# Query projection of a perceiver block: its first group moved ahead of the branch, with a new order of fetches

## The chip, the cores and the metric

The kernel runs on one core of a Trainium2 chip. The metric is the device time of one execution in microseconds; three runs of the kernel before gave a median of 925.47 us (925.44 to 926.23). The core's engines are TensorE (PE, with its weight loads PEld), VectorE (DVE), ScalarE (ACT), GpSimd (POOL) and SyncE (SP). SP does no arithmetic here: it issues transfers. ACT can issue transfers as well.

## What is computed

One perceiver block on 32 sequences of 64 tokens of width 512, all in f32: a cross-attention over a context of 1601 rows with a mask, a causal self-attention, and a feed-forward with ternary weights. Each is added to its input. The change touches the first of the three:

```python
mn = _rmsnorm(mem_seq, rms_scale)
xn = _rmsnorm(x, rms_scale)             # x comes in already layer-normed
q = jnp.einsum('BTD,NDH->BTNH', xn, q_w)          # 4 heads of 128
kv = jnp.einsum('BSD,cKDH->cBSKH', mn, kv_w)
q = _apply_rope(q, q_pos) * HEAD_DIM ** (-0.5)
k = _apply_rope(k, k_pos)
logits = jnp.einsum('BTKGH,BSKH->BKGTS', q, k)
masked = jnp.where(mem_mask[:, None, None, None, :], logits, MASK_FILL)
probs = jax.nn.softmax(masked, axis=-1)
enc = jnp.einsum('BKGTS,BSKH->BTKGH', probs, v)
return jnp.einsum('BTNH,NHD->BTD', enc, out_w)    # added to x
```

## The kernel before, in words

**Opening (L262 to L358).** The kernel first ranks the 32 sequences by how many of their context rows are not masked. A copy turns the mask to f32 (L308), two matmuls count (L314), DVE compares the counts with `steps` (L321) and reduces them to a rank (L330 to L343), two matmuls put the ranks in order (L345, L346), and `ints` receives the order and the flag `fits` (L352, L353). Beside that the query weights `wq` are scaled, and their column mean taken away: `each` (L292), four matmuls `wmean` (L297), four DVE operations in place (L301). `wq` and the later output weights share the tile `wo`. POOL scales `wkv` (L358).

**Branch.** If the ranks fit a fixed plan of lengths (they do in this profile), `cross_last` runs, which reads only the last rows that each sequence needs, two sequences to a pair, 16 pairs; otherwise `cross_all`. Every engine loads `fits` and branches.

**Queries (`query_steps`, L193 to L252).** The 2048 tokens are taken in four groups of 512. For group g: four raw tiles `xres[2..5]` give mean and variance on DVE (`spread_of`, L207 and L208, four pairs), `deviations` (L214 on DVE, L215 on POOL) turns them into a factor per token, `tables` makes four diagonal blocks `eye` on DVE (L221), spreads them over all partitions by a matmul with ones (`rb`, L223), and multiplies the result with cosine and sine (L225, L226). Each of the four heads is four matmuls (L248) of `wq` with `wide(g)`, the transposed tokens in `xres[8..11]` or `[12..15]`. `rotate` then copies the halves across on ACT (L231, L232) and has three DVE operations (L234 to L236), the last of which writes `qT_all`. `eye` shares its place, `xres[6]`, with the cosine table, so the next group's `eye` is made after the last rotation that reads the table. Each f32 matmul is two instructions in the trace.

**Order.** `cross_last` interleaves by hand: group 0, group 1, group 2 with `project(0, j)` (keys and values of pair 0, L486) after each head, group 3. After them come `inverse_rms(1)` (L468 on DVE, L469 on POOL) and `add_mask(1)`, then the loop over pairs. Its first stage, p = 1, runs `project(1, 0..2)`, `turn_keys(0)`, `project(1, 3)`, `logits(0, 0)` (L528), `project(1, 4)`. Results of `project` leave PSUM through ACT with the pair's `rstd` (L493). SP is one queue in order: it issues `ct` and mask (`load_rest`), tokens, context rows `nat` (`load_rows`, 8 buffers, freed by `square` on ACT), the queries of a pair back from `qT_all` (`fetch_queries`), the output weights, and pieces of the feed-forward weights, whose absolute sums `magnitude` takes on DVE (L1035). `in_order` pins the program order of the named engines.

Of the kernel before, what the change touches and what calls it, by code (L numbers as in the profile page):

```python
# [80 lines left out]
def perceiver_kernel(ctx: ExitStack, tc: tile.TileContext, a: dict, out: bass.AP):  # L81
# [91 lines left out]

    GQ = 4 * P

    def raw(t):
        return xres[:, 2 + t % 4]
# [4 lines left out]
    def fetch_wide(g, queues):  # L182
        src = a["xT"].rearrange("(c p) t -> p c t", p=P)[:, :, g * GQ : (g + 1) * GQ]
        for k, queue in enumerate(queues):
            part = slice(k * DC // len(queues), (k + 1) * DC // len(queues))
            queue.dma_start(wide(g)[:, part], src[:, part])

    def fetch_raw(t):
        nc.sync.dma_start(raw(t), x_in[t * P : (t + 1) * P, :])

    def query_steps(psq, psr, pool):

        S8 = GQ // T  # L193
        qcos = pool.tile([P, T], F32, name="qcos")
        qsin = pool.tile([P, T], F32, name="qsin")
        nc.sync.dma_start(qcos, a["qcos"])
        nc.sync.dma_start(qsin, a["qsin"])
        cosr, sinr = (xres[:, k].rearrange("p (b t) -> p b t", t=T) for k in (6, 7))
        eye = xres[:, 6].rearrange("p (t q) -> p t q", q=P)
        over = lambda v: v.unsqueeze(1).to_broadcast([P, S8, T])  # L200
        mvs, rss = {}, {}

        def spread_of(g, k):
            if k == 0:
                mvs[g] = small.tile([P, 4, 2], F32, tag="qmv", name=f"qmv_{g}")
            st = small.tile([P, 6], F32, tag="stats", name=f"stats_q{g}_{k}")
            nc.vector.bn_stats(st, raw(4 * g + k))  # L207
            nc.vector.bn_aggr(mvs[g][:, k], st)  # L208

        def deviations(g):  # L210


            rs = small.tile([P, 4], F32, tag="qrs", name=f"qrs_{g}")
            nc.vector.tensor_scalar(rs, mvs.pop(g)[:, :, 1], 1.0 + 1e-6, 1e-11, ALU.mult, ALU.add)  # L214
            nc.gpsimd.tensor_tensor(rs, rs, neghalf[:, :4], ALU.pow)  # L215
            rss[g] = rs

        def tables(g):
            rs = rss.pop(g)
            for k in range(4):  # L220
                nc.vector.tensor_scalar(eye[:, k], ident, rs[:, k : k + 1], None, ALU.mult)  # L221
            rb = psr(f"rb_{g}")
            nc.tensor.matmul(rb, ones, xres[:, 6], start=True, stop=True)  # L223
            rb = rb.rearrange("p (b t) -> p b t", t=T)
            nc.vector.tensor_tensor(cosr, rb, over(qcos), ALU.mult)  # L225
            nc.vector.tensor_tensor(sinr, rb, over(qsin), ALU.mult)  # L226

        def rotate(g, h, ps):
            u = pool.tile([P, S8, T], F32, tag="u", name=f"qu_{g}_{h}")
            t = norm.tile([P, D], F32, tag="xn", name=f"qt_{g}_{h}")  # L230
            nc.scalar.copy(t[:H], ps[H:])  # L231
            nc.scalar.copy(t[H:], ps[:H])  # L232
            t = t.rearrange("p (b t) -> p b t", t=T)
            nc.vector.tensor_tensor(u, ps.rearrange("p (b t) -> p b t", t=T), cosr, ALU.mult)  # L234
            nc.vector.tensor_tensor(t, t, sinr, ALU.mult)
            nc.vector.tensor_tensor(qT_all[:, S8 * g : S8 * (g + 1), h, :], u, t, ALU.add)  # L236

        groups = NT // 4
        for g in range(groups):
            if g == 0:  # L240
                for k in range(4):
                    spread_of(0, k)
                deviations(0)
            mid, made = (2 if g == 0 else 1), []
            for h in range(NH):
                ps = psq(h, f"q_{g}_{h}")
                for c in range(DC):
                    nc.tensor.matmul(  # L248
                        ps, wq[:, c, h, :], wide(g)[:, c], start=(c == 0), stop=(c == DC - 1)
                    )  # L250
                made.append((h, ps))
                if h == mid:  # L252
                    tables(g)
                if h >= mid:
                    for k, ps in made:
                        rotate(g, k, ps)
                        if g + 1 < groups:
                            spread_of(g + 1, k)
                    made = []
                if h == NH - 1 and g + 1 < groups:  # L260
                    deviations(g + 1)
                yield  # L262


    with ExitStack() as st:
        r1 = st.enter_context(tc.tile_pool(name="r1", bufs=1))
        ps_r = st.enter_context(tc.tile_pool(name="ps_r", bufs=2, space=PSUM))
        ps_w = st.enter_context(tc.tile_pool(name="ps_w", bufs=1, space=PSUM))
        m8 = r1.tile([P, B, NC], U8, name="m8")
        table = r1.tile([B, 5, B], F32, name="table")  # L270
        steps = r1.tile([B, 2, NC], F32, name="steps")

        nc.scalar.dma_start(m8, a["maskE"])
        nc.scalar.dma_start(scale1, a["rms"])
        for c in range(DC):
            (nc.scalar if c % 2 else nc.sync).dma_start(
                wq[:, c], a["L0_xattn_q_w"].rearrange("h (c p) k -> p c h k", p=P)[:, c]
            )
        nc.scalar.dma_start(steps, a["steps"])
        nc.scalar.dma_start(table, a["rank"])  # L280
        fetch_wide(0, [nc.sync, nc.scalar, nc.sync, nc.scalar])
        for t in range(4):
            fetch_raw(t)
        for k in range(2):
            nc.scalar.dma_start(
                wkv[:, :, k], a["L0_xattn_kv_w"][k, 0].rearrange("(c p) h -> p c h", p=P)
            )
        nc.vector.tensor_scalar(scale1, scale1, 1.0, None, ALU.add)

        def centre_weights():  # L290
            each = r1.tile([P, DC, P], F32, name="each")
            nc.vector.tensor_scalar(  # L292
                each, scale1.unsqueeze(2).to_broadcast([P, DC, P]), 1.0 / D, None, ALU.mult
            )
            mean = ps_w.tile([P, D], F32, name="wmean")
            for c in range(DC):
                nc.tensor.matmul(  # L297
                    mean, each[:, c], wo[:, c], start=(c == 0), stop=(c == DC - 1)
                )
            for c in range(DC):  # L300
                nc.vector.scalar_tensor_tensor(  # L301
                    wo[:, c], wo[:, c], scale1[:, c : c + 1], mean, ALU.mult, ALU.subtract
                )

        def ranks():

            mf = r1.tile([P, B, NC], F32, name="mf")
            nc.vector.tensor_copy(mf, m8)  # L308

            halves = r1.tile([B, B, 2, NC], F32, name="halves")  # L310
            for k in range(2):
                part = slice(k * T, (k + 1) * T)
                count = ps_r.tile([P, B, NC], F32, tag="r", name=f"count_{k}")
                nc.tensor.matmul(  # L314
                    count[:B].rearrange("p b c -> p (b c)"),
                    ones[part, :B],
                    mf[part].rearrange("p b c -> p (b c)"),
                    start=True,
                    stop=True,
                )  # L320
                nc.vector.scalar_tensor_tensor(  # L321
                    halves[:, :, k],
                    count[:B],
                    0.0,
                    steps[:, k].unsqueeze(1).to_broadcast([B, B, NC]),
                    ALU.is_gt,
                    ALU.mult,
                )
            need = r1.tile([B, B], F32, name="need")
            nc.vector.tensor_reduce(need, halves.rearrange("p b k c -> p b (k c)"), AX.X, ALU.max)  # L330

            key = r1.tile([B, B], F32, name="key")
            nc.vector.scalar_tensor_tensor(key, need, float(B), table[:, 0], ALU.mult, ALU.add)
            own = r1.tile([B, B], F32, name="own")
            nc.vector.tensor_tensor(own, key, table[:, 1], ALU.mult)
            mine = r1.tile([B, 1], F32, name="mine")
            nc.vector.tensor_reduce(mine, own, AX.X, ALU.add)
            above = r1.tile([B, B], F32, name="above")
            nc.vector.tensor_scalar(above, key, mine, None, ALU.is_gt)
            rank = r1.tile([B, 1], F32, name="rank")  # L340
            nc.vector.tensor_reduce(rank, above, AX.X, ALU.add)
# [37 lines left out]
    def cross_last():  # L379
# [63 lines left out]
        def load(p):  # L443
            load_rest(p)
            load_rows(p, range(tiles(p)))
# [1212 lines left out]
```

## Time and profile before

| | us |
|---|---|
| median of three runs | 925.47 |
| the profiled execution | 926.73 |
| its span, first to last instruction | 924.5 |
| PE busy (4518 matmul instructions) | 889.0 |
| DVE, ACT, POOL busy | 630.9, 371.4, 70.9 |
| mean granted PE clock | 0.991 |
| transfers, whole span | 87.92 MB, mean 95 GB/s |

The profiled execution is 1.26 us above the median, and 2.2 us of it lie outside the span. A row of the timeline gives start, length, engine, line, operation, result and operands, and in brackets the idle time of the engine before it and what ended it. In the tables by stretch the busy time of each engine stands with the granted clock (1.00 is full speed) and the share and rate of the transfer engines.

### The profile page before, as it was taken

What the parts mean: (1) busy time and instruction counts of PE and PEld (TensorE: products, weight loads), DVE (VectorE), ACT (ScalarE), POOL (GpSimd) and SP (SyncE); (2) the same over time, 40 slices, a digit from 0 to 9 for tenths busy, and PEclk for the clock granted to TensorE, in tenths of its full rate; (3) what the DMA queues carried; (4) which work ended last, traced back from release to release, by engine and by line L of the source; (5) the groups of instructions that cost most, each with busy time, mean ns of one, the idle gap of its engine ahead of it and who ended that gap; (6) DMA issues with size and microseconds to landing.
All of it is one profiled execution on the core that took longest, in us unless ns stands there. A gap on an engine that the chain in (4) does not pass through costs nothing.

```text
span 924.5 us, 12905 instructions
## 1 busy us (share of the span) xinstructions
PE 889.0 (96%) x4518; PEld 633.5 (69%) x4518; DVE 630.9 (68%) x1215; ACT 371.4 (40%) x790; POOL 70.9 (8%) x83
## 2 busy tenths in 40 slices
PE   6799999999999998999999999999999999999997
PEld 2355777777777765666676666666668878878886
DVE  5587566565456563478898898877866775886864
ACT  0424645554455532122222322223554555554551
POOL 2010211111111100000000000000001000000000
PEclk8999999999999999999999999999999999999999
DMA  8874898777557560011111001000000020020111
GB/s 258 248 222 129 246 254 250 219 244 228 174 174 222 146 216 26 1 35 35 47 51 41 24 24 46 24 24 1 1 1 1 0 46 1 1 46 1 23 23 51
DMA packets 63123, 87.92 MB, mean 95 GB/s; under 512 B 11172, under 2 KB 34248, under 8 KB 63048
## 3 DMA queue, kind: packets, MB, share of 16 engines
q1 hardware_dynamic: 59648, 84.79, 31.2%
q10 hardware_dynamic: 3400, 2.20, 0.8%
q8 instruction: 38, 0.62, 0.3%
q14 instruction: 37, 0.30, 0.1%
HBM read 78.58 MB, written 4.19 MB: 90 GB/s over the span
## 4 chain that ended last, share of the span: by engine, by line
PE 71%; DVE 21%; issue 3%; ACT 3%; DMA 1%; POOL 1%; ACTq 0%; DVEq 0%; POOLq 0%
PE y L1465 13%; PE kvp L486 13%; PE fh L1122 11%; PE xo L608 6%; PE aV L1212 5%; PE q L248 4%; DVE s L1260 4%; PE enc L592 4%; PE lgp L528 3%; DVE amx L1269 2%; DVE s L1270 2%; DVE s L1280 2%; DVE atot L1278 2%; PE aptp L1290 1%; PE sc L1255 1%
## 5 line engine op out<-in xcount | busy, mean ns | idle before, releaser
L486 PE MATMUL kvp<-wkv,ct 128*128 128x256 f32 x576 | 135.0, 380 | 1.8 <-ACT kv L493 1.7
L486 PEld LDWEIGHTS kvp<-wkv,ct 128*128 128x128 f32 x576 | 106.9, 190 | 23.9 <-issue 9.3
L1465 PE MATMUL y<-wp,hTh 128*128 128x512 f32 x236 | 94.4, 400 | 0.4 <-DVE xres L1442 0.4
L1465 PE MATMUL y<-wp,hTl 128*128 128x512 f32 x236 | 92.8, 393 | 0.0
L1122 PE MATMUL fh<-fxh,wf 128*128 128x512 f32 x256 | 71.6, 401 | 1.3 <-DVE mv_f L128 0.9
L1122 PE MATMUL fh<-fxl,wf 128*128 128x512 f32 x256 | 70.5, 397 | 0.0
L493 ACT ACTIVATE kv<-kvp,rstd 128x256 f32<-128x256 f32 x72 | 34.0, 472 | 89.6 <-PE kvp L486 80.4
L1130 ACT ACTIVATE bank<-fh 128x512 f32<-128x512 f32 x64 | 38.1, 596 | 78.7 <-PE fh L1122 78.7
L248 PE MATMUL q<-xres,wo 128*128 128x512 f32 x128 | 59.8, 623 | 2.4 <-DVE wo L301 2.4
L1317 PE MATMUL aout<-bank,aoT 128*128 128x512 f32 x128 | 60.9, 620 | 1.1 <-ACT aoT L1311 1.1
L1200 PE MATMUL aWQ<-axT,bank 128*128 128x256 f32 x256 | 58.0, 380 | 2.9 <-POOL wo L1166 1.8
L535 DVE CUSTOM_DVE_ANT_0 pr<-lgp,bias 128x384 f32<-128x384 f32 (+6 forms) x64 | 28.4, 458 | 47.4 <-PE lgp L528 47.0
L1200 PEld LDWEIGHTS aWQ<-axT,bank 128*128 128x128 f32 x256 | 48.5, 190 | 15.4 <-issue 6.2
L608 PE MATMUL xo<-wo,encT 128*128 128x512 f32 x128 | 57.9, 594 | 1.1 <-ACT encT L601 1.1
L1460 DVE SCALAR_TENSOR_TENSOR hTl<-bank,lnw,hTh 128x512 fp32r<-128x512 f32 x59 | 44.0, 750 | 20.7 <-ACT hTh L1459 20.7
L1200 PE MATMUL aWK<-axT,bank 128*128 128x256 f32 x256 | 57.9, 379 | 0.0
L1212 PE MATMUL aV<-bank,axT 128*128 128x512 f32 x128 | 57.6, 594 | 0.0
L1122 PEld LDWEIGHTS fh<-fxl,wf 128*128 128x128 f32 x256 | 48.3, 189 | 11.2
L1122 PEld LDWEIGHTS fh<-fxh,wf 128*128 128x128 f32 x256 | 46.7, 188 | 13.2 <-issue 2.2
L1465 PEld LDWEIGHTS y<-wp,hTh 128*128 128x128 f32 x236 | 44.3, 188 | 14.0 <-DVE xres L1442 3.4
L1200 PEld LDWEIGHTS aWK<-axT,bank 128*128 128x128 f32 x256 | 48.6, 190 | 6.6
L1273 ACT ACTIVATE s<-s 128x1024 f32<-128x1024 f32 x16 | 16.9, 1058 | 90.2 <-DVE s L1270 90.2
(164 smaller groups left out, 1487.9 us busy)
## 6 DMA issues: line engine op xcount, KB each, us to landing
nat<-in_ctx_dram SPq DMA_DIRECT2D x64, 256.0 KB, 4.4
ct<-in_ctxT_dram SPq DMA_DIRECT2D x7, 768.0 KB, 4.4
xres<-in_x_dram SPq DMA_DIRECT2D x16, 256.0 KB, 4.7
xres<-in_x_dram SPq DMA_DIRECT2D x32, 128.0 KB, 5.6
qs<-bank SPq DMA_DIRECT2D x32, 128.0 KB, 4.8
raw_g<-in_W_fcT_dram SPq DMA_DIRECT2D x16, 256.0 KB, 4.5
raw_g<-in_W_projT_dram SPq DMA_DIRECT2D x16, 256.0 KB, 4.5
raw_q<-in_W_fcT_dram SPq DMA_DIRECT2D x16, 256.0 KB, 2.9
```

What stands on the lines that cost most here:

```text
L248: nc.tensor.matmul(ps, wq[:, c, h, :], wide(g)[:, c], start=(c == 0), stop=(c == DC - 1))
L486: nc.tensor.matmul(ps.rearrange("p k h -> p (k h)"), cts[p][:, c, j * P : (j + 1) * P], wkv[:, c].rearrange("p k h -> p (k h)"), start=(c ...
L592: nc.tensor.matmul(encs[s], kv[row : row + w, j, 1], pT[row : row + w, j], start=(done == 0), stop=(done + w == n),)
L608: nc.tensor.matmul(o, encT[:, h].rearrange("p s t -> p (s t)"), wo[:, h, :], start=(h == 0), stop=(h == NH - 1),)
L1122: nc.tensor.matmul(ps, wf[:, c, cols], part[:, c, :], start=(i == 0 and c == 0), stop=(i == 1 and c == DC - 1),)
L1130: nc.scalar.activation(g, ps, AF.Gelu)
L1200: nc.tensor.matmul(ps[:, m, :], ws[w][:, c, (m0 + m) * P : (m0 + m + 1) * P], xT[:, c, :], start=(c == 0), stop=(c == DC - 1),)
L1212: nc.tensor.matmul(ps, xT[:, c, i * P : (i + 1) * P], ws["WV"][:, c, :], start=(c == 0), stop=(c == DC - 1),)
L1260: nc.vector.scalar_tensor_tensor(s[half], sc[half, :, :, half].rearrange("p r m k -> p (r m) k"), DK**-0.5, cmask[half].unsqueeze(1).to_br ...
L1317: nc.tensor.matmul(ps, oT[:, c, :], ws["WO"][:, c, :], start=(c == 0), stop=(c == DC - 1))
L1460: nc.vector.scalar_tensor_tensor(lo, g, w, hi.bitcast(F32), ALU.mult, ALU.subtract)
L1465: nc.tensor.matmul(y, part[:, t, :], wp[:, c, :], start=(c == 0 and i == 0), stop=(c == FC - 1 and i == 1),)
```

## The change

The first group of queries, with all its tables and rotations, and the statistics and tables of group 1, now stand in the opening, ahead of the branch. The opening's PSUM pools are four banks for heads, two for `wmean` and `rb`, two for the ranks, at the places where `cross_last` has its pools. `eye` moves to `xres[0]` and the rotation's scratch to `xres[1]`; `diagonals` makes `eye` on ACT, for the next group, in the middle of the present one. `each` and the scaling of `wkv` go from DVE and POOL to ACT. The mask, the ranking table and the steps come in one transfer (`opening`); `xT`, `wq` and `wkv` are laid out by the host so that each partition reads one run. The raw tiles come in two transfers of two tiles each. In `cross_last`, the rows of a pair are fetched ahead of its `ct`, the tokens of pairs 0 and 1 only at the end of stage p = 1, `inverse_rms(1)` moves into group 2, and the loads of the output weights and of the first two pieces move into stage p = 1. The pieces' sums then run two later, to p = 16. The opening is pinned on SP too.

The core of the diff:

```diff
+    eye, turn = xres[:, 0], xres[:, 1].rearrange("p (b t) -> p b t", t=T)
-    def fetch_raw(t):
-        nc.sync.dma_start(raw(t), x_in[t * P : (t + 1) * P, :])
+    def fetch_raw(g):
+        for k in (0, 2):
+            src = x_in[(4 * g + k) * P : (4 * g + k + 2) * P, :]
+            nc.sync.dma_start(xres[:, 2 + k : 4 + k], src.rearrange("(t p) d -> p t d", p=P))
+    def diagonals(g):
+        rs = rss.pop(g)
+        for k in range(4):
+            part = slice(k * P, (k + 1) * P)
+            nc.scalar.activation(eye[:, part], ident, AF.Copy, scale=rs[:, k : k + 1])
+    def tables(g, qrot, rb):
+        nc.tensor.matmul(rb, ones, eye, start=True, stop=True)
...
+        for g in range(1, GROUPS):
+            more = g + 1 < GROUPS
+            if g > 1:
+                tables(g, qrot, psr(f"rb_{g}"))
             for h in range(NH):
+                rotate_query(g, h, query(g, h, psq(h, f"q_{g}_{h}")))
+                if more and h < 2:
+                    spread_of(g + 1, 2 * h)
+                    spread_of(g + 1, 2 * h + 1)
+                if more and h == 1:
                     deviations(g + 1)
+                if more and h == 2:
+                    diagonals(g + 1)
+                yield g, h
...
+        nc.sync.dma_start(opening, a["opening"])
         nc.scalar.dma_start(scale1, a["rms"])
+        for k in (0, 2):
+            nc.sync.dma_start(wo[:, k : k + 2], a["wq"][:, k : k + 2])
+        nc.vector.tensor_copy(mf.rearrange("p b c -> p (b c)"), m8)
+        nc.vector.tensor_scalar(scale1, scale1, 1.0, None, ALU.add)
+        nc.scalar.activation(
+            each, scale1.unsqueeze(2).to_broadcast([P, DC, P]), AF.Copy, scale=1.0 / D
+        )
+        fetch_wide(0, [nc.scalar, nc.scalar])
+        nc.scalar.dma_start(wkv, a["wkv"])
+        fetch_raw(0)
+        qrot = fetch_rotations(r1)
...
+        query(0, 0, heads[0])
...
+        for k in range(4):
+            spread_of(0, k)
+        deviations(0)
+        diagonals(0)
         for c in range(DC):
+            nc.scalar.activation(wkv[:, c], wkv[:, c], AF.Copy, scale=scale1[:, c : c + 1])
+        query(0, 1, heads[1])
+        fetch_raw(1)
+        fetch_wide(1, [nc.sync])
+        for k in range(4):
+            spread_of(1, k)
+        deviations(1)
+        query(0, 2, heads[2])
+        tables(0, qrot, ps_b.tile([P, GQ], F32, tag="b", name="rb_0"))
+        query(0, 3, heads[3])
+        for h in range(NH):
+            rotate_query(0, h, heads[h])
+            if h == 1:
+                diagonals(1)
+        tables(1, qrot, ps_b.tile([P, GQ], F32, tag="b", name="rb_1"))
+        in_order(begin, (Engine.PE, Engine.DVE, Engine.Activation, Engine.Pool, Engine.SP))
...
+        few = NATS - tiles(0)
+        load_rows(0, range(tiles(0)))
+        fetch_raw(2)
+        fetch_wide(2, [nc.sync])
+        load_rest(0)
+        load_rows(1, range(few))
+        for g, h in queries:
+            if (g, h) == (1, 1):
+                fetch_raw(3)
+                load_rest(1)
                 for j in range(tiles(0)):
                     square(0, j)
+                load_rows(1, range(few, tiles(1)))
+            if (g, h) == (1, 2):
+                inverse_rms(0)
+                add_mask(0)
+            if (g, h) == (1, 3):
+                fetch_wide(3, [nc.sync])
+            if g == 2:
+                for j in range(h * tiles(0) // NH, (h + 1) * tiles(0) // NH):
+                    project(0, j)
+            if (g, h) == (2, 1):
                 for j in range(tiles(1)):
                     square(1, j)
+                load_rows(2, range(tiles(2)))
+            if (g, h) == (2, 2):
+                inverse_rms(1)
+                add_mask(1)
+            if (g, h) == (2, 3):
+                cts.pop(0)
+                rotate(0)
+                load_rest(2)
         fetch_queries(0)
-        tc.keep_in_program_order(load_output_weights())
-        for j in range(2):
-            magnitude(j, load_piece(rawp, j, "g"))
...
             if now:
-                fetch_queries(p)
                 free = min(later, NATS - ahead)
                 if later:
                     load_rows(p + 2, range(free))
-                raws = [load_piece(rawp, j, "g") for j in (2 * p, 2 * p + 1)]
+                if p == 1:
+                    load_output_weights()
+                fetch_queries(p)
+                raws = [load_piece(rawp, 2 * p - 2 + k, "g") for k in range(2)]
...
+            if p <= NT:
+                for k, r in enumerate(raws):
+                    magnitude(2 * p - 2 + k, r)
...
                 if later:
                     load_rest(p + 2)
+                if p == 1:
+                    for v in range(4):
+                        load_tokens(v // 2, v % 2, sequence(v))
                 if p == NT - 1:
+                    raws = [load_piece(rawp, 2 * p + k, "g") for k in range(2)]
                     load_attention_weights()
```

## The prediction

> **What bounds the kernel now.** I read the summary first, then the table by stretch, then the timeline of the first 120 us. PE is busy nearly throughout; in the 40 slices (23.1 us each) only the first two lie below 9, and the first alone has a lowered clock.
>
> ```profile
> PE 889.0 (96%) x4518; PEld 633.5 (69%) x4518; DVE 630.9 (68%) x1215; ACT 371.4 (40%) x790; POOL 70.9 (8%) x83
> PE   6799999999999998999999999999999999999997
> PEclk8999999999999999999999999999999999999999
> ```
>
> So what can be won lies in about the first 95 us. The table by stretch (us; busy time and count of PE, PEld, DVE, ACT, POOL; granted clock, share and GB/s of the transfers) shows it: PE idles 8.75 us in the first stretch and 4.63 in the third, and runs at 0.80 in the second; from 100 us on it idles 0.24 us in 40.
>
> ```profile
> 0.00:15.30 15.30, 6.55 (x17) 1.95 (x17) 7.27 (x23) 0.00 (x0) 0.70 (x6) 0.95 0.79 245
> 15.30:28.25 12.95, 12.95 (x24) 5.56 (x25) 4.45 (x14) 3.60 (x5) 4.66 (x5) 0.80 0.92 284
> 28.25:45.90 17.65, 13.02 (x29) 5.44 (x28) 13.08 (x27) 7.53 (x16) 1.01 (x1) 0.96 0.73 236
> 100.00:140.00 40.00, 39.76 (x182) 30.33 (x182) 28.39 (x79) 22.28 (x66) 6.95 (x7) 1.00 0.92 262
> ```
>
> The timeline names the waits. The first head starts at 15.29, behind a chain that begins with a small transfer (`steps`, landed at 8.9 though issued at 3.29), runs through DVE and ends with `ints`. The next table matmul waits 4.63 us for `eye`, and `project(1, 2)` waits 1.71 us for the scale of pair 1.
>
> ```profile
> 8.95 1.08 DVE L321 SCALAR_TENSOR_TENSOR halves<-count,steps 32x416 f32<-32x416 f32 x2 [3.95 <-DMA steps<-in_steps_dram]
> 14.12 0.13 DVE L353 CAST ints<-fit 1x1 int32<-1x1 f32 x1
> 15.29 13.13 PE L248 MATMUL q<-xres,wo 128*128 128x512 f32 x24 [2.43 <-DVE wo L301]
> 28.25 1.02 PE L223 MATMUL rb<-xres,ones 128*128 128x512 f32 x2
> 44.21 1.92 PE L223 MATMUL rb<-xres,ones 128*128 128x512 f32 x2 [4.63 <-DVE xres L221]
> 45.93 11.40 PE L248 MATMUL q<-xres,wo 128*128 128x512 f32 x24
> 57.17 1.89 PE L486 MATMUL kvp<-wkv,ct 128*128 128x256 f32 x8
> 89.83 3.62 PE L486 MATMUL kvp<-wkv,ct 128*128 128x256 f32 x16
> 95.15 1.99 PE L486 MATMUL kvp<-wkv,ct 128*128 128x256 f32 x8 [1.71 <-ACT kv L493]
> 99.45 1.67 PE L528 MATMUL lgp<-kT,qs 128*128 128x448 f32 x4
> ```
>
> At full clock one matmul instruction of 512 columns starts 0.43 us after the last (weight loads from 21 to 39 us). The 24 from 15.29 to 28.25 took 12.96 instead of 10.3: **2.6 us of slow clock**. After the idle 4.63, the two `rb` took 1.72 instead of 0.86 and the next 24 took 11.24 instead of 10.3: **1.8 us**. I follow one mark, the first `lgp`, at 99.45.
>
> **Part 1: the opening.** Added up on the rows: the mask landed 2.52 us after its issue; with the tables beside it I take 3.4 (absolute). DVE: cast 0.38, `scale1` 0.17, to 4.0. `each` is now ACT's first operation, so the table load (1.28, the row at 21.64, which there too came after the wait) stands before it: 5.3, and 0.6 for 512 columns: 6.0. If the load runs early this is 4.7, but then the second half of `wq` (0.15 + 1.05 MB at 0.35 MB/us from 2.3) holds `wmean` to about 5.7, so 0.3 at most is won. The eight `wmean` instructions need 3.4 us warm and up to 5.4 if the clock stays low to 10; they end at 9.7 to 11.4, and 0.1 + 0.66 later the first corrected block lets the heads start: **10.6 to 12.3; I take 11.5**. The tokens: `fetch_wide(0)` stands on ACT behind `each`; issued from 6.0, behind 3.3 MB in all at 0.28 to 0.38 MB/us (the rates from 3 to 13 us), its halves land near 10.4 and 11.7, and are needed at 11.5 and 13.2. So: 15.29 - 11.5 = **3.8 us gained**, and the rank chain, `fits` and `ints` leave the path: they lie beside the heads. PE now idles under 2 us between `wmean` and the heads, where it idled 4.7; the clock should hold: **2.6 gained** (none, if it falls).
>
> **Part 2: the table gap.** `eye` of group 1 is made in the opening, so the 4.63 and its 1.8 go: **6.4 gained**. What is late next is `eye` of group 2, made behind DVE's backlog. From DVE's first `wo` correction at 10.7: corrections 2.7, fit and `ints` 0.6, four statistics 3.3, `deviations` 0.2, to 17.5. The raw pairs of group 1 can be issued on SP only when two statistics are done (15.7 and 17.4), and land 3.5 later (the shortest landing 2.0, and 0.52 MB at 0.35): statistics from 19.2 to 22.5, 22.7 with `deviations`. `rb_0` is done then (11.5 + 24 x 0.43 + 0.9 = 22.7). Tables 1.2, four rotations of 1.92 (30.52 to 32.44) 7.7, tables 1.2, DVE's own branch 0.4, two rotations each with two statistics 2 x 3.56, `deviations` 0.2: 40.5. POOL 1.1. Four `diagonals` on ACT: no row, but Exp of 128 x 128 takes 392 ns and a 128 x 256 copy 364, so 0.37 each, 1.5: `rb_2` at 43.1. PE arrives at 11.5 + 32 x 0.43 + 4 x 0.43 + branch 0.6 + 32 x 0.43 = 41.3. **A gap of 1.8 comes back.** DVE moves with PE's start, so this hardly depends on 11.5; bounds 0 and 2.5. `eye` moved off DVE is 0.9 a group there; ACT has idle time for it (7.5 busy of 17.65), and for `wkv` (4 x 0.47, beside the heads).
>
> Does the gap cost clock? In the trace 4.63 us of idling brought a slow stretch, and 1.71 at 93.4 none (1.00 in every us from 92 to 102); 1.8 lies by the second. [...] By the longer gap's row 1.8 would be added; I leave it out of the sum and keep it in the range.
>
> **Part 3: the branch in mid-stream.** From `ints` (14.25) to SP's next transfer 0.74, to PE's next weight load 1.0. PE's sequencer can run ahead under `rb_1`, so between 0 and 1.0: **0.6 lost**. Behind it `q(1, 0)` writes a bank that rotation (0,0) has left (about 25); heads 1, 2, 3 need banks left by rotations (0,2), (0,1), (0,3), at 28 to 31, before they are due.
>
> **Part 4: pair 0 to p = 1.** From group 2 on PE needs 5.16 us a head and DVE 3.6, so nothing waits. The factor of pair 1 is ready a group early: from the end of `q(3,3)` to `lgp` it was 9.62 (89.83 to 99.45), and the work in it is 4 x 1.73 + 0.55 = 7.5: **2.1 gained**. What is late next is `qs`, read back from `qT_all`: last rotation 3.4 after the last head (93.26 less 89.83), transfers of 2.0 to 4.5 after issue: the first half at 5.5, just in time; by the upper end 0.5 is lost.
>
> **Part 5: transfers and the rest, at nothing.** SP's order past the branch: rows of pair 0, raw and wide of group 2, `ct_0`, rows of pair 1: some 7.4 MB from 17.5, at 0.35 by 39; `ct_0` is needed at 48, `wide(2)` at 43. `raw(3)`, `ct_1`, `wide(3)` follow from 37 and are needed from 49 on. `fetch_queries(0)` blocks SP as before; behind it rows, output weights, `qs`, pieces and `ct_3` make 4.8 MB, 18 us at 0.28, and `ct_3` is due 22 us after `qT_all` is done. The tokens of pairs 0 and 1, 0.5 MB (1.9 us), now fall into that busy stretch (share 0.92); SP waits there 8.0 us in 80 for PE to free `ct`, so there is room, but if not it costs up to 1.9. The two late sums (1.27 on DVE at p = 16) lie in a 2.9 us idle of DVE before 354.17; the attention weights are issued about 14 us later on SP, after 343, and 4.7 MB at 0.33 bring the first by 350, where they are needed at 363.7 (times of the trace before).
>
> **The sum**: -3.8 - 2.6 - 6.4 + 1.8 + 0.6 - 2.1 = **-12.5 us**. The profiled execution, 926.73, would be 914.2; on the median of 925.47 it is **913.0**.
>
> **Rivals.**
> 1. *No gap comes back* (DVE faster than its rows, start at 10.6): 1.8 and 0.9 more, 910.3. For it: DVE's chain has 1.7 of pure waiting for raw pairs. Against: every other link is a measured row.
> 2. *The new PSUM pools wait for the old as a whole*, so that the change doesn't do what its banks are laid out for: `q(1,0)` waits for DVE's last table at 33 instead of 27.5; the gap at `rb_2` shrinks by 1.8, and an idle of 5.5 brings 1.8 of slow clock: +5.5, 918.5. For it: nothing in the trace shows a pool's hand-over. Against: in the trace before, `wkv` is scaled on POOL from 15.39 to 19.0 while PE is past the branch, so waits cross it one by one.
> 3. *Slow clock remains* in group 0 or after `rb_2`: +1.8 to 2.6, 915 to 915.6.
> 4. *Slower: transfers become the bound* in pairs 1 to 4. By 140 us 31.7 MB were moved (the table's rates); PE would want them by 127.5, 254 GB/s from 2.5 us on. While busy at 0.92 they gave 262, and SP holds `ct` back for buffers. If the mean is only 228 (that of the first 160 us), they take 139 and all is given back; below 228 the kernel is slower, at 220 by 4 us (930). Against: the rate reaches 400 in unhindered stretches, and 31% of the first 95 us is unused.
>
> **How the numbers follow.** Forecast (911.5 to 914.8) 0.52; rival 1 (909 to 911.5) 0.13; rival 3 0.12 and rival 2, with losses on transfers, together up to 919.5, 0.12; most of the gain given back but still faster 0.04; within 0.2% (1.85 us, what a measurement of this kernel can tell from no change) 0.03; rival 4 0.04. The low end is the start at 10.6, no gap, no branch cost and an early table load (913.0 - 0.9 - 1.8 - 0.6 - 0.3 = 909.4, rounded down); the high end rival 2 with half of the token cost.
>
> **What would show it.** Right: first head at 10.6 to 12.3, clock 1.00 through group 0; `rb_1` with no idle; `rb_2` with 0 to 2.5 idle, released by ACT's `eye`; no wait before `project(1, 2)`; first `lgp` near 87, and PE over 99% busy from there. Wrong: `q(1,0)` released by DVE, PE waiting for a transfer (`ct`, `nat`, `qs`), or the same 40 us after 100 showing more idle than 0.3.

## The result and the profile after

The changed kernel takes 920.2 us in the median of four runs (917.5 to 920.37), the kernel before 925.46: a ratio of 0.9929, interval 0.9916 to 0.9942. It is faster, by 5.3 us on the medians; 12.5 were forecast, with a likely band of 911.5 to 914.8 and rivals up to 919.5. The median of 920.2 lies 0.7 above all of it; by the ratio (0.9929 of 925.47 is 918.9) the time lies just inside, where rival 2 was put. The profiled execution after is the shortest of the four, 917.5 us with a span of 915.7.

First the lines of the summary that were read before:

```profile
PE 884.7 (97%) x4518; PEld 632.3 (69%) x4518; DVE 628.4 (69%) x1198; ACT 378.7 (41%) x811; POOL 67.1 (7%) x79
PE   7899999999999999999999999999999999999997
PEclk9999999999999999999999999999999999999999
```

The work of PE is the same (4518 instructions), and the first two slices are fuller, but still not full. Then the same four stretches of the table, with the same columns:

```profile
0.00:15.30 15.30, 9.84 (x23) 3.63 (x24) 8.42 (x25) 1.91 (x2) 0.70 (x6) 1.00 0.74 254
15.30:28.25 12.95, 12.71 (x30) 5.32 (x28) 9.79 (x23) 7.63 (x18) 2.04 (x2) 1.00 0.90 302
28.25:45.90 17.65, 13.62 (x28) 6.04 (x29) 12.59 (x23) 6.94 (x15) 0.00 (x0) 0.90 0.81 269
100.00:140.00 40.00, 39.76 (x179) 29.40 (x178) 26.36 (x69) 20.27 (x58) 5.91 (x6) 1.00 0.90 253
```

In the first stretch PE is busy 9.84 instead of 6.55, in the second it gets through 30 instructions at full clock instead of 24 at 0.80. The third is where the gain stops: PE idles 4.03 of 17.65, nearly as long as the 4.63 before, and the clock is lower (0.90 against 0.96). From 100 to 140 PE idles 0.24 us, as before. PE's timeline says what the third stretch waits for:

```profile
5.60 5.06 PE L314 MATMUL wmean<-wo,each 128*128 128x512 f32 x8 [0.56 <-DMA wo<-in_wq_dram]
12.32 10.54 PE L231 MATMUL q<-xres,wo 128*128 128x512 f32 x24 [1.46 <-DMA xres<-in_xT_dram]
22.70 1.02 PE L224 MATMUL rb<-xres,ones 128*128 128x512 f32 x2
26.99 1.02 PE L224 MATMUL rb<-xres,ones 128*128 128x512 f32 x2
32.27 15.67 PE L231 MATMUL q<-xres,wo 128*128 128x512 f32 x32 [4.26 <-DVE xres L240]
48.97 1.13 PE L224 MATMUL rb<-xres,ones 128*128 128x512 f32 x2 [1.03 <-ACT xres L215]
85.17 5.34 PE L502 MATMUL kvp<-wkv,ct 128*128 128x256 f32 x24
92.51 1.67 PE L544 MATMUL lgp<-kT,qs 128*128 128x448 f32 x4
```

`rb_1` (26.99) follows without idle: the table gap is gone. Behind it stands a new one of the same size: `q(1,0)`, the first head beyond the branch, waits 4.26 us for a DVE operation of line 240, the first of a rotation. DVE's timeline tells which rotation:

```profile
24.96 0.68 DVE L240 TENSOR_TENSOR xres<-q,xres 128x512 f32<-128x512 f32 x1
31.33 0.69 DVE L240 TENSOR_TENSOR xres<-q,xres 128x512 f32<-128x512 f32 x1
39.09 0.69 DVE L240 TENSOR_TENSOR xres<-q,xres 128x512 f32<-128x512 f32 x1 [4.54 <-ACT qt L238]
```

The first row is the first operation of line 240 and belongs to rotation (0,0); that of 31.33 is the fourth, belongs to rotation (0,3), and ends at 32.02, 0.25 before PE starts. The bank that `q(1,0)` writes was left by rotation (0,0), which had read it by 25.7. The last row shows the price on the other side: DVE then idles 4.54 until `q(1,0)` is there. The mark, the first `lgp`, comes at 92.51 instead of 99.45, 6.94 earlier. Nearly all of the rest of the 8.8 in the span is one slow stretch of PE's clock, 1.7 us, that the profile before has at 682 to 686 and this one has not.

Such stretches make one run differ from the next, so the experiments below are compared by their medians and ratios to runs of the kernel before on the same chip, and by marks inside the first 100 us.

### The profile page after: what moved, and what is told of

The parts are those of the page before. It is cut to its first block, busy times and chain, and to the rows that moved or that the text cites. A ratio compares the mean times of both kernels' runs of the same rounds, so it can differ in the third digit from the quotient of the medians.

```text
span 915.7 us, 12886 instructions
## 1 busy us (share of the span) xinstructions
PE 884.7 (97%) x4518; PEld 632.3 (69%) x4518; DVE 628.4 (69%) x1198; ACT 378.7 (41%) x811; POOL 67.1 (7%) x79
## 4 chain that ended last, share of the span: by engine, by line
PE 73%; DVE 21%; ACT 3%; issue 1%; DMA 1%; POOL 0%; ACTq 0%; DVEq 0%; POOLq 0%
PE kvp L502 14%; PE y L1481 13%; PE fh L1138 11%; PE xo L624 6%; PE aV L1228 5%; PE q L231 5%; DVE s L1276 4%; PE enc L608 4%; PE lgp L544 3%; DVE amx L1285 2%; DVE s L1286 2%; DVE s L1296 2%; DVE atot L1294 2%; PE aptp L1306 2%; PE sc L1271 1%; PE pt L593 1%
## 5 line engine op out<-in xcount | busy, mean ns | idle before, releaser
L1311 ACT COPY wo<-aptp 64x256 f32<-64x256 f32 x64 | 23.3, 365 | 72.2 <-PE aptp L1306 55.0
```

## The experiments

**1. The same kernel again**, for a second profile and five more runs. No edit.

> The changed kernel, unchanged, several times over. Its four runs were 917.5 once (mean clock 0.997, the profiled one) and 920.1 to 920.4 three times (0.992). Theory A: the two levels are the place of the slow-clock stretches only; a stretch is about 3.4 us long and costs 1.7 to 1.9 us, so the runs fall on levels some 1.8 to 2.7 apart, the lower clock always with the longer time, and a profiled execution near 920 shows one or two slow stretches more than the one at 32 to 36 us, at the same order of work. Rival: another wait comes and goes (a transfer); then the longer execution shows more idle PE at the same clock.

Measured: 920.27 (919.62 to 921.42), ratio 0.9934 (0.9921 to 0.9948).

```profile
32.94 16.66 PE L231 MATMUL q<-xres,wo 128*128 128x512 f32 x32 [4.28 <-DVE xres L240]
```

The wait is there again, 4.28, with the same releaser. The 32 instructions behind it took 16.66 instead of 15.67: this time the clock was at half for 6.8 us, from 31.5, of which 5.4 fell on them; in the first profile it was 3.4 us. The first head started at 12.95 and the first `lgp` at 94.16, 5.3 before that of the kernel before; the medians differ by 5.3 in the first measurement and by 6.3 in this one. The two spans of the changed kernel, 915.7 and 919.0, differ by 3.3: 0.6 is the later start, 1.0 the longer slow clock here, and 1.7 a further slow stretch at 677 to 680. So theory A holds but for the start. The clocks of the other runs (0.992 or 0.993, against 0.997 in the first profile) suggest that this is the usual case.

**2. Two heads into other banks (kvbank).** `q(1,0)` and `q(1,1)` write the banks of `ps_kv`, which lie over the two that the ranks used; the others stay.

```diff
             lambda h, name: (
-                ps_pt.tile([P, 2, NQ], F32, tag="pt", name=name).rearrange("p l q -> p (l q)")
+                ps_kv.tile([P, GQ], F32, tag="kv", name=name)
+                if name in ("q_1_0", "q_1_1")
+                else ps_pt.tile([P, 2, NQ], F32, tag="pt", name=name).rearrange("p l q -> p (l q)")
```

> Heads 0 and 1 of group 1 are put into the banks of the key-value pool, which lie on those of the ranks (left at about 14 us). Theory A: after the branch the first head waits for the last PSUM reader of the whole old pool of heads, rotation (0,3), not for its own bank; so here it starts at 28.0 to 28.5 instead of 32.3, the idle 4.3 and the slow stretch of 1.8 behind it go, DVE's rotations of group 1 start at about 34.6 instead of 39.1, and the third table matmul moves from 49.0 to about 44.5, with 2 to 2.5 us of idle PE ahead of it (2 heads' worth of DVE backlog). First logits at about 88.0 instead of 92.5; the time falls by 4 to 5 us, to 915.5 to 916 beside 920. Rival: the wait is for something else past the branch (rotations done, tables of group 1, or the branch itself); then the first head stays at 32 and the time within 0.5 of the changed kernel's.

Measured: 915.05 (913.18 to 916.77), ratio 0.9879 (0.9864 to 0.9895).

```profile
28.19 13.90 PE L231 MATMUL q<-xres,wo 128*128 128x512 f32 x32
44.68 1.13 PE L224 MATMUL rb<-xres,ones 128*128 128x512 f32 x2 [2.60 <-ACT xres L215]
```

The first row has no bracket: no idle between `rb_1` and `q(1,0)`, though the branch lies between them. So the branch costs PE nothing that can be seen here, and the banks were the whole wait. The 32 now take 13.90, at full clock. The gap at `rb_2` is larger than in the kernel after, 2.60 instead of 1.03, since PE arrives earlier; the first `lgp` comes at 88.22.

**3. The same banks, declared one by one (split_pools).** Is it the pool? Here each head writes the same bank as in the kernel after; only the declaration differs.

```diff
-        ps_q = st.enter_context(tc.tile_pool(name="ps_q", bufs=4, space=PSUM))
+        ps_h = [
+            st.enter_context(tc.tile_pool(name=f"ps_q{h}", bufs=1, space=PSUM)) for h in range(NH)
+        ]
```

> After with nothing changed but the declaration of the opening's PSUM banks for heads: four pools of one bank each instead of one pool of four; the banks stay the same, q(1,0) still writes a bank that a head of group 0 left. Theory A (a new pool waits for the last reader of every old pool that it lies over, as a whole): the pool of q(1,0) now lies over the banks of heads 0 and 1 alone, so it waits for the first DVE operation of rotation (0,1), over at 27.8, and PE arrives at 27.9; q(1,1) waits for rotation (0,3) and is due at 31.4, so 0.5 to 1 us of idle there. The 4.4 idle goes, the slow clock with it, first lgp at 88 to 89, 914.5 to 916.5. Theory B (what q(1,0) waits for is the branch or DVE's backlog, not the pool): idle of 4 us before q(1,0) as in after, 920.

Measured: 915.4 (914.45 to 916.93), ratio 0.9878 (0.9862 to 0.9893).

```profile
29.32 3.67 PE L231 MATMUL q<-xres,wo 128*128 128x512 f32 x8 [0.59 <-DVE xres L240]
33.48 10.54 PE L231 MATMUL q<-xres,wo 128*128 128x512 f32 x24 [0.49 <-DVE xres L240]
28.38 0.69 DVE L240 TENSOR_TENSOR xres<-q,xres 128x512 f32<-128x512 f32 x1
```

The 4.3 has become 0.59 before `q(1,0)` and 0.49 before `q(1,1)`, both for the same line of DVE: in rotation (0,1) it ends at 29.07 (the last row), in rotation (0,3) at 33.34, 0.25 and 0.14 ahead of PE. That is the pattern that a wait for whole pools gives: the new pool of `q(1,0)` lies over the old banks 0 and 1, that of `q(1,1)` over 2 and 3, and each waits for the last reader of what it lies over. The bank that `q(1,0)` itself writes had been read by rotation (0,0) at 26.95, 2.1 us before the wait ended.

**4. Work to keep the clock up (warm).** Dummy matmuls, whose results nobody reads: eight of 128 columns at the start, four ahead of the first head, four of 512 between `rb_1` and the branch.

```diff
+        for _ in range(4):
+            nc.tensor.matmul(spare, ones, eye, start=True, stop=True)
```

> Matmuls whose results nobody reads are added in the idle times of PE: eight of 128 columns at the start, four of 128 columns between the ranks and the first head, four of 512 columns between the second table and the branch. They change no order. Theory A (slow clock is a cost of its own, 1.7 to 1.9 per stretch): the stretch at 32 to 36 goes, the first head of group 1 still starts at about 32.3, first logits at about 90.7 instead of 92.5 (2.5 to 3 if a stretch at the start is saved in common runs as well), and the runs scatter less; 917.5 to 918.5 beside 920.2. Rival: the idle time itself is the cost and the clock follows from the rows only by chance: no change within 0.5, or a loss of up to 1 if the eight first matmuls delay the counts.

Measured: 915.18 (914.66 to 917.53), ratio 0.9877 (0.9861 to 0.9892).

```profile
27.99 3.60 PE L375 MATMUL spare<-xres,ones 128*128 128x512 f32 x8
32.42 13.97 PE L231 MATMUL q<-xres,wo 128*128 128x512 f32 x32 [0.84 <-DVE xres L240]
```

`q(1,0)` starts at 32.42, as late as in the kernel after, so the wait is untouched; but the 32 take 13.97 instead of 15.67 to 16.66. The slow clock is a cost of its own behind the wait, 1.7 to 2.7 us, and filling the hole with empty work saves it. The median fell by 5.1, more than expected and as much as in kvbank and split_pools, where the wait is gone, so the medians alone don't tell the two apart; the rows do. On the mark (90.96) it is 1.6 to 3.2 earlier than in the two profiles of the kernel after; where the rest of the 5.1 comes from isn't settled, since the profiled run is the longest of the four.

**5. Eye late (kv_late_eye).** kvbank with the diagonals of group 1 behind all rotations of group 0: part 2 of the change undone.

```diff
         for h in range(NH):
             rotate_query(0, h, heads[h])
-            if h == 1:
-                diagonals(1)
+        diagonals(1)
```

> kvbank with the diagonals of group 1 made after all rotations of group 0 instead of in the opening: it prices the part of the change that takes away the table gap. Theory A (the gap was a true wait for eye): rb_1 waits 3.5 to 5 us for ACT at about 27, the first lgp comes 2 to 5 us later than in kvbank (the idle at rb_2, 2.6 there, takes up part of it; slow clock adds 1.7 if it falls): 917 to 920. Theory B (the wait would only have moved to the rotations or banks behind it): lgp within 1 us of kvbank's 88.2, 914.5 to 916.

Measured: 919.84 (919.12 to 920.66), ratio 0.9928 (0.9913 to 0.9943).

```profile
33.05 2.07 PE L224 MATMUL rb<-xres,ones 128*128 128x512 f32 x2 [5.94 <-ACT xres L215]
```

The table gap is back, 5.94, longer than expected, with 6.8 us of slow clock that begins inside it (30.1 to 36.9). The first `lgp` comes 6.1 after kvbank's (94.36), the time is 4.8 more. The forecast for part 2 was 6.4, or 4.6 after the gap of 1.8 that comes back at `rb_2`. So it is worth about what was forecast, and it was a true wait.

**6. Pair 1's factor late (late_rstd).** `inverse_rms(1)` and `add_mask(1)` back behind group 3: part 4 undone.

```diff
-            if (g, h) == (2, 2):
-                inverse_rms(1)
-                add_mask(1)
...
+        inverse_rms(1)
+        add_mask(1)
         fetch_queries(0)
```

> The scales and the mask of pair 1 are made after group 3 again, as before the change; nothing else differs from the changed kernel. By part 4 of the prediction project(1, 2) waits again for about 1.7 us and first logits come 1.7 to 2.1 later (94.2 to 94.6 instead of 92.5 in an execution with the same slow stretches); 922 beside 920.2. Rival: the queries read back from memory would have been late by then anyway, so that less than 0.5 shows.

Measured: 921.72 (921.25 to 923.52), ratio 0.9955 (0.994 to 0.9971).

```profile
91.83 1.99 PE L502 MATMUL kvp<-wkv,ct 128*128 128x256 f32 x8 [1.75 <-ACT kv L509]
```

The wait before `project(1, 2)` returns, 1.75 against 1.71. From the end of `q(3,3)` to the first `lgp` it is 9.67 us (86.46 to 96.13) instead of 7.34: 2.3, of which the median shows 1.5.

**7. The layouts alone (layout_only).** The kernel before with the new host layouts, the one opening transfer and the new first fetches, with group 0 still behind the branch and `each` still on DVE.

```diff
-        for c in range(DC):
-            (nc.scalar if c % 2 else nc.sync).dma_start(
...
-        fetch_wide(0, [nc.sync, nc.scalar, nc.sync, nc.scalar])
+        nc.sync.dma_start(opening, a["opening"])
+        for k in (0, 2):
+            nc.sync.dma_start(wo[:, k : k + 2], a["wq"][:, k : k + 2])
+        fetch_wide(0, [nc.scalar, nc.scalar])
```

> Before with the new host layouts, the single opening transfer, the two-tile raw fetches of group 0 and the order of the first fetches alone; group 0 of queries stays behind the branch and each keeps its place on DVE. Theory A (the chain that set the first head hung on the small transfer steps, and the transfers need about 12 us for what the first head reads): steps no longer ends last, the first head starts at 12.3 to 13.3 instead of 15.29, released by DVE's corrections of wo or by the tokens; the slow stretch from 15 us on goes or shrinks; the 4.63 at the second rb and the 1.71 before project(1,2) stay. Gain 2 to 5.5 us: 920 to 923, that is, much or all of what the whole change gained net. Theory B (the gain at the start came from taking the branch out of the chain): the first head stays near 14.5 to 15.3, the gain is below 1 us.

Measured: 924.49 (923.48 to 926.75, 11 runs), ratio 0.9982 (0.9973 to 0.9991). The profiled run is the one of 926.75.

```profile
7.56 6.69 PE L292 MATMUL wmean<-wo,each 128*128 128x512 f32 x8 [2.23 <-DVE need L325]
17.21 12.15 PE L247 MATMUL q<-xres,wo 128*128 128x512 f32 x24 [2.76 <-DVE wo L296]
```

Both theories missed the first head, which starts later than before, at 17.21 instead of 15.29; the gain, 2.3 on the medians and 1.7 by the ratio, is at or just below the lower end of theory A, which put it at 2 to 5.5. The eleven runs fall into two groups, six at 923.5 to 924.5 and five at 926.1 to 926.8; the profile is of the later group, and how the others start isn't known. `steps` is off the path (its operation runs at 5.36 instead of 8.95), but `wmean` starts at 7.56 and takes 6.69 for eight instructions, 0.84 each: half rate to its end. `need` (over at 7.48) is named, but it feeds no operand of `wmean`; what `wmean` reads last is `wq`, whose transfers took 7.2 us here and 4.3 in the kernel after. One thing that differs is ACT's ring, the queue of the transfers that ACT issues: here it issues the tokens at 1.21; in the kernel after it does so at 3.51, behind `each`. This run alone does not show that the 7.2 comes from there; the next one tests it.

**8. Tokens early (kv_early_tokens).** That reading, tried on kvbank: the tokens of group 0 issued before `each`.

```diff
+        fetch_wide(0, [nc.scalar, nc.scalar])
         mf = r1.tile([P, B, NC], F32, name="mf")
...
-        fetch_wide(0, [nc.scalar, nc.scalar])
```

> kvbank with the tokens of group 0 issued on ACT's ring before the scale factors are awaited (at about 1.2 instead of 3.5). Theory A (read from layout_only: tokens issued that early share the rate with wq on SP's ring, and wmean, which stands first, gets its weights later): wq lands at 7 instead of 5.6, wmean runs at the cold rate of 0.85 us each to about 14, the first head starts at 14 to 15 instead of 12.7, 916 to 918. Theory B (the branch alone made layout_only late, the order of issue doesn't matter): start at 12 to 12.8, 914 to 915.5.

Measured: 918.71 (917.45 to 919.42), ratio 0.9909 (0.9893 to 0.9924).

```profile
7.43 6.35 PE L314 MATMUL wmean<-wo,each 128*128 128x512 f32 x8 [2.38 <-DMA wo<-in_wq_dram]
14.61 10.57 PE L231 MATMUL q<-xres,wo 128*128 128x512 f32 x24 [0.64 <-DVE wo L334]
47.82 2.08 PE L224 MATMUL rb<-xres,ones 128*128 128x512 f32 x2 [3.12 <-ACT xres L215]
```

Now the row itself names `wq`: it comes 1.7 later than in kvbank (5.74), `wmean` runs slowly nearly to its end, and the first head starts at 14.61 instead of 12.66. So 1.9 of the 2.6 us that kvbank's start lies ahead of the kernel before hang on the order of issue, with the tokens held back behind `each`; the layouts and leaving out the branch, without that order, leave 0.7. Only the order of issue differs: with the tokens on ACT's ring issued at 1.20 instead of 3.50, `wq` on SP's ring comes the 1.7 us later. The idle at `rb_2` grew to 3.12, and 6.8 us of slow clock came with it, which was not expected; the time is 0.7 above the range given.

**9. Raw tiles last (kv_rawlast).** kvbank with the raw tiles of group 0 on ACT's ring behind the tokens.

```diff
+        fetch_raw(0, nc.scalar)
         nc.scalar.dma_start(wkv, a["wkv"])
-        fetch_raw(0)
```

> kvbank with the raw tiles of group 0 issued on ACT's ring behind the tokens, not on SP's ring beside them. Theory A (the first head waits because the tokens, issued at 3.5, share the engines with the raw tiles issued on SP): the tokens land 0.7 to 1.3 us earlier, the first head starts at 11.4 to 12.0, then released by DVE's corrections of wo, time 913.8 to 914.5. Theory B (the engines' total rate and wmean set the start anyway): start at 12.3 or later, 915 to 916.

Measured: 917.69 (916.14 to 918.3), ratio 0.9897 (0.9882 to 0.9912).

```profile
5.55 6.64 PE L314 MATMUL wmean<-wo,each 128*128 128x512 f32 x8 [0.52 <-DMA wo<-in_wq_dram]
13.03 10.57 PE L231 MATMUL q<-xres,wo 128*128 128x512 f32 x24 [0.64 <-DVE wo L334]
```

The tokens are no longer waited for (6.5 us to land instead of 9.7), as theory A had it, yet the start is later: all eight of `wmean` ran at half rate, 6.64, and then DVE's corrections were last. `rb_2` idled 3.13, again with 6.8 us of slow clock. On the medians it is 2.6 slower than kvbank, 1.7 above the upper end of theory B, which had the start right (12.3 or later); by the ratios it is 1.7 slower, and their intervals overlap.

**10. Statistics first (kv_stats_first).** kvbank with all statistics of the next group ahead of rotation (g,0), and the diagonals after rotation (g,1).

```diff
             for h in range(NH):
+                if more and h == 0:
+                    for k in range(4):
+                        spread_of(g + 1, k)
+                    deviations(g + 1)
                 rotate_query(g, h, query(g, h, psq(h, f"q_{g}_{h}")))
-                if more and h < 2:
-                    spread_of(g + 1, 2 * h)
-                    spread_of(g + 1, 2 * h + 1)
                 if more and h == 1:
-                    deviations(g + 1)
-                if more and h == 2:
                     diagonals(g + 1)
```

> kvbank with all four statistics and the deviations of the next group ahead of rotation (g,0), and the diagonals behind rotation (g,1). Theory A (the idle at rb_2, 2.60 in kvbank and 1.03 in after, stems from DVE's order: statistics behind rotations): the idle falls below 0.5, the first lgp comes at 85.6 to 86.5, time 912.5 to 913.5. Theory B (DVE's backlog as a whole sets it, or the raw pairs land too late): rotations are pushed back, q(2,0) or rb_2 waits as long for its banks, lgp at 88 or later, 915 to 917.

Measured: 912.41 (911.18 to 912.99), ratio 0.9841 (0.9828 to 0.9855).

```profile
28.27 1.12 PE L224 MATMUL rb<-xres,ones 128*128 128x512 f32 x2 [1.05 <-ACT xres L215]
43.03 1.02 PE L224 MATMUL rb<-xres,ones 128*128 128x512 f32 x2
87.88 1.74 PE L543 MATMUL lgp<-kT,qs 128*128 128x448 f32 x4 [1.00 <-DMA qs<-bank]
```

The gap at `rb_2` is gone, so DVE's order made it. In this profile two other waits took its place: `rb_1` 1.05, since the raw tiles of group 1 landed late (DVE waited 1.55 and 2.35 us for them), and the first `lgp` 1.00, since the queries read back were not there. The mark is only 0.34 earlier than kvbank's, while the median is 2.6 lower; the profiled run is the longest of its five, and kvbank's the shortest. One source of such differences can be seen in the profiles: from the first `lgp` to the end they take 823.2 to 823.5 us, or 824.7 to 825.1 where a slow stretch falls between 665 and 686 us, so that stretch alone moves a run by 1.7 us. Kvbank's profile has none, and its median run has a span 1.7 longer. That this is all of the 2.6 is not shown, since the other runs have no profile.

**11 and 12. Together.** stats_warm is kv_stats_first with the two sets of short dummy matmuls; combined has the raw tiles last as well.

```diff
+        early = ps_r.tile([P, P], F32, tag="r", name="early")
+        for _ in range(8):
+            nc.tensor.matmul(early, ones, ones, start=True, stop=True)
         nc.sync.dma_start(opening, a["opening"])
```

> kv_stats_first with eight dummy matmuls of 128 columns at the start and four behind the ranks, as in warm. Theory A (wmean runs at half rate until PE has been busy for some us, which costs up to 1.7): wmean takes 4.3 instead of 5.6, the first head starts at 11.6 to 12.4, then released by the tokens; rb_1 waits 1 to 1.9 for the raw tiles of group 1, so most of it is lost there; first lgp at 87 to 88, 911.5 to 912.5, that is, 0 to 0.9 below kv_stats_first. Theory B (the dummies delay count or wmean): 912.5 or more.

> stats_warm with the raw tiles of group 0 behind the tokens on ACT's ring. Theory A (in kv_rawlast the tokens did land earlier, at about 11, and only wmean at its cold rate kept the first head at 13.0): with the dummies the first head starts at 11.2 to 11.7, released by DVE's corrections; 0 to 0.9 below stats_warm, if the statistics of group 1 don't take it back. Theory B (the raw tiles of both groups come later and hold back rb_1 and rb_2): idle at rb_1 of 1.5 to 3, at or above stats_warm, 912 to 914.

Measured: stats_warm 911.63 (909.61 to 912.41), ratio 0.9832 (0.9818 to 0.9846); combined 910.79 (909.14 to 912.36), ratio 0.9829 (0.9815 to 0.9844). The two can't be told apart by time. In stats_warm the first head starts at 12.75, later than expected, since `wmean` waits 0.62 for the second half of `wq` and the head 0.69 for the tokens. The timeline of combined:

```profile
6.42 3.83 PE L316 MATMUL wmean<-wo,each 128*128 128x512 f32 x8
11.38 10.46 PE L231 MATMUL q<-xres,wo 128*128 128x512 f32 x24
26.52 1.13 PE L224 MATMUL rb<-xres,ones 128*128 128x512 f32 x2 [0.38 <-ACT xres L215]
41.21 1.02 PE L224 MATMUL rb<-xres,ones 128*128 128x512 f32 x2
84.89 1.67 PE L549 MATMUL lgp<-kT,qs 128*128 128x448 f32 x4
```

`wmean` takes 3.83 instead of 6.64: with PE warm, the raw tiles' place pays at the start after all. The first head starts at 11.38 instead of 12.75 in stats_warm, and the mark is 0.8 earlier. Combined beats the kernel before by 1.7% and, by the ratios, the kernel after by about 1% (0.9829 against 0.9934).

## Why the prediction was right in direction and wrong in size

The terms on the mark, first `lgp`; the last column is the second profile, taken to stand for the usual run:

| term | on record | profile after | again |
|---|---|---|---|
| start of the first head | -3.8 | -2.97 | -2.34 |
| slow clock in group 0 | -2.6 | -2.6 | -2.6 |
| table gap and its clock | -6.4 | -6.4 | -6.4 |
| gap at `rb_2` | +1.8 | +1.0 | +1.0 |
| branch in mid-stream | +0.6 | 0 | 0 |
| banks of group 1: idle | 0 | +4.3 | +4.3 |
| their slow clock (32 instructions above 13.90) | 0 | +1.8 | +2.8 |
| pair 1's factor | -2.1 | -2.3 | -2.3 |
| sum | -12.5 | -7.2 | -5.5 |
| measured on the mark | | -6.9 | -5.3 |

**The step that failed** is in part 3: "`q(1, 0)` writes a bank that rotation (0,0) has left (about 25); heads 1, 2, 3 need banks left by rotations (0,2), (0,1), (0,3), at 28 to 31, before they are due." The bank was free, but the wait was not for the bank: it was for the last reader in the pool of four, rotation (0,3). kvbank and split_pools both remove it, and take 915.05 and 915.4 instead of 920.27. It was on record as rival 2, at +5.5 and with a share of a 0.12; measured, it is 4.3 of idle, 1.8 to 2.8 of clock, less 0.8 at `rb_2` beside the forecast gap of 1.8: 5.3 to 6.3. Less the 1.6 by which the gap is really larger without the wait (2.60 in kvbank for 1.03), it is 4.5 to 5.5, and kvbank's median is 5.2 lower. So its price was right and its chance too small. What spoke against it, that POOL scaled `wkv` while PE was past the branch, showed how a wait crosses a branch, not what a new pool over old banks waits for; no row of the trace before showed that.

**Part 1** was right that the chain through `steps` goes, and a little short of its size: 12.32 and 12.95 for 11.5, the upper end of the range and beyond. Two links were late. `wmean` took 5.06 and 6.25, and the tokens, put at 10.4 for the first half, were still waited for at 12.3. The tokens took 9.3 us to land, while SP's ring had a megabyte of raw tiles under way beside them; with these behind them it was 6.5 (kv_rawlast). The table load did run early (at 1.20), and `each` was done at 4.1 instead of 6.0; as forecast, `wq` then set `wmean`, at 5.60.

**Part 2** stands: no idle at `rb_1`, and 5.94 when the part is undone. At `rb_2` 1.03 instead of 1.8, because DVE, waiting for `q(1,0)`, had caught up; without that wait the gap is 2.60 (kvbank), just above the bound of 2.5. **Part 3**'s 0.6 for the branch is 0 (in kvbank `q(1,0)` follows `rb_1` without idle, at 28.19). **Part 4** stands, at 2.3 for 2.1. **Part 5** at nothing holds: the 40 us from 100 show 0.24 of idle, as before, and the difference of 6.9 on the mark is still 6.9 when the self-attention begins (356.76 for 363.71). Rival 4 is thus excluded here. **Rival 3**, slow clock in group 0 or behind `rb_2`, came in neither place in the two profiles of the kernel after, but behind the wait of `q(1,0)`.

The high end, 919.5, allowed for rival 2 with 1.0 of other losses; the start took 0.8 to 1.5 and the second slow stretch of the usual run 1.0, and together they passed it on the medians. That the result comes near the range at all is due to this allowance for rival 2, not to the forecast itself, whose band ends at 914.8.

## What to carry to other kernels

When PSUM pools are laid over old ones, ask at which grain the new one waits: here the first tile waited for the last reader of the whole old pool, and four pools of one bank instead of one of four took nearly all of that away (4.3 us of idle became 1.1) with no other change. A stall that is removed shows what stands behind it: follow the next waits with each engine's own order, down to the one that a new hand-over adds. And a transfer that is issued earlier on a second queue can delay the one that is needed first: `wq` came 1.7 us later beside tokens issued 2.3 us earlier (kv_early_tokens), and the tokens landed in 6.5 us instead of 9.7 with the raw tiles behind them (kv_rawlast).

## What the runs showed of the chip, not expected

- **Clock after idling.** In the first 100 us of these profiles a single idle of PE of 2.60 us or less behind steady work never lowered the clock, and every one of 3.12 or more did (3.12, 3.13, 4.21, 4.26, 4.28, 4.28, 4.63, 5.94). In the opening, where PE had worked little before, the clock fell at less: at 17.1 us in an idle of 2.76 in layout_only, and in the kernel before at 13.7, after an idle of 2.29 and within one of 2.43, with only four short matmuls between. The slow time in these 100 us was 3.4 or 6.8 us, nothing between, and so cost up to 1.7 or 3.4; in kv_late_eye, for one, it began 2.9 us before PE was back. No idle between 2.60 and 3.12 behind steady work occurred, so what one of that length does isn't shown.
- **Half rate in the opening.** In the kernel after the granted clock reads 1.00 throughout the opening, yet the first instructions of `wmean` come 0.85 us apart and later ones 0.43 (in kv_rawlast, at the same reading, all eight stay slow, to 12.2). There the spacing of the instructions is the evidence, not the column. Dummy matmuls in the first 5 us shortened `wmean` from 6.64 (kv_rawlast) to 3.83 (combined).
